# Attention of a graph network on one core: groups of four chunks in an order fixed by the source

## The chip, the core and the metric

The kernel runs on one core of a Trainium2 chip. A core has five engines, each with its own queue of instructions that it works off in order: TensorE (PE in the profile; PEld is its loading of weights), VectorE (DVE), ScalarE (ACT), GpSimd (POOL) and SyncE (SP). They wait for each other through semaphores. Data moves between the memory of the chip and the core's SBUF by DMA; transfers with an index per row (gathers) are issued by POOL, plain ones here by SP and ACT. The time is that of one execution on the device in microseconds, the median of several runs.

## The reference, cut to what matters

6250 nodes have 256 features each; 106,250 edges (50,000 drawn ones in both directions and a loop at each node) are sorted by destination. Two blocks follow each other, each with a layer norm and a relu ahead and a residual behind. The first is three layers of a relational network. The second, which the change touches, is graph attention:

```
h = x @ Wv + bv
q, k = h @ wq + bq, h @ wk + bk
e = q[src] + k[dst]
c = where(e > 0, e, 0.2 * e)
m = segment_max(c, dst);  ex = exp(c - m[dst])
attn = ex / segment_sum(ex, dst)[dst]
out = x + segment_sum(h[src] * attn[:, None], dst)
```

## The kernel before

The edges are cut into 831 chunks of 128. 56 windows of destination nodes take 15 chunks each (47 of them) or 14 (nine); a window holds at most 128 nodes, and the last chunk of the window in front is looked at again for the edges that spill over, so 15 or 16 chunks are used in a window (`refs`). If the input doesn't have the order that this needs, a general path runs instead; for this input `ordered_path` runs.

Three layers come first. In each, POOL gathers for every chunk the 128 source rows (`msg`, L719), DVE builds a 0/1 matrix of edge against node and type (`hot`), and TensorE sums with it (L852) and multiplies by the weights (L790). The last layer also leaves a table `hx` in memory: for each node its 256 values of `h` and its `q`.

Attention goes over the same chunks and windows with the line L719 gathering `head`, 128 rows of `hx`, 48 buffers deep. For a window:

- For each chunk DVE compares a row of numbers with the edges' local destinations (`other`, L911: 1 where the edge does not end at the node), ACT makes `qm` from it (L918: `other` times -1e30 plus `q` of the edge's source, so that edges of other nodes vanish in the exponent), and TensorE turns it (L920) so that nodes lie on partitions. Up to four chunks share a bank `pq` of PSUM, the accumulating memory; three such banks take turns.
- For each group of four: ACT writes 0.2 times the logits to `c` (L923), DVE takes the maximum into `tops` (L924) and puts the larger of the logit and its fifth into `c` (L925).
- Four small DVE steps make the guard of the exponent from `tops` (L928 to L931), then ACT takes the exponent of the whole window in one pass and sums it (L933).
- For each group: TensorE turns the weights back (`pe`, L938), DVE (even groups) or ACT (odd groups) copies them to SBUF (`ex`, L943 and L941), and TensorE multiplies them with the heads and sums over all chunks in `po` (L945; each of these matmuls is two passes in the profile).
- DVE divides by the sum and adds the window's rows of x (`y`, L951). SP loads those rows (`xt`, L916) and stores the result (L953), both at an address that it reads from `first`, a word which DVE writes after the first `other` of the window (`at_base`, L722 to L728).

The source says this window by window. The order of instructions on each engine isn't that of the source: a planner with assumed costs orders each stage by priority, and puts semaphores where data or buffers ask for them. In the order that it made for attention, the queues hold the `other` and `qm` of the next window between the parts of the present one, and on TensorE the turning back of three groups in a row, then their sums in one run of 24 passes, then the last group.

Of the kernel before, what the change touches and what calls it, by code (L numbers as in the profile page):

```python
# [19 lines left out]
P = 128  # L20
KS = 19
NO_NODE = 1 << 20
MASKED = -1.0e30
FLOOR = -1.0e29
EPS = 1e-5
SLOPE = 0.2
# [403 lines left out]
def kernel(  # L430
# [19 lines left out]
    nc = tc.nc  # L450
    N, D = x.shape
# [3 lines left out]
    HX = D + 1  # L455
# [3 lines left out]
    NW = -(-NC // CW)  # L459
# [3 lines left out]
    sizes = [CW] * NLONG + [CW - 1] * NS  # L463
    first_c = [sum(sizes[:t]) for t in range(NW)]
# [3 lines left out]
    groups = [list(range(g, min(g + 4, NT))) for g in range(0, NT, 4)]  # L468
# [33 lines left out]
    with tc.tile_pool(name="prep", bufs=1) as prep, \  # L502
# [49 lines left out]
        for at, view, k in by_window(dst_t):  # L552
# [36 lines left out]
        for to, of, b in ((loc_p, dst_t, base_b), (seg_p, seg_t, seg_b)):  # L589
# [15 lines left out]
                                op0=ALU.mult, op1=ALU.add)  # L605
        nc.vector.tensor_reduce(viol[:, 1:2], scr[:, :full], AX.X, ALU.max)
        if rest:
            nc.vector.tensor_copy(viol[:rest, 2:3], over[:rest, full:full + 1])
            nc.vector.tensor_scalar(viol[:rest, 3:4], seg[:rest, full:full + 1], -1.0, -0.5,
                                    op0=ALU.mult, op1=ALU.add)  # L610
# [17 lines left out]
                                op0=ALU.mult, op1=ALU.add)  # L628
# [39 lines left out]
    with tc.tile_pool(name="nw", bufs=3) as nw:  # L668
# [3 lines left out]
        for ts in groups:  # L672
            n = len(ts)
            xt = nw.tile([P, 4, D], F32, name="xt")
# [32 lines left out]
    def ordered_path():  # L707
# [5 lines left out]
        up = cps.tile([P, WMAX], F32)  # L713
        nc.vector.tensor_copy(up, up_s)
        k_n = cst.tile([P, NW], F32)
        bs = path.enter_context(tc.tile_pool(name="bs", bufs=3))

        def gather(to: bass.AP, table: bass.AP, index: bass.AP):
            nc.gpsimd.indirect_dma_start(  # L719
                out=to, out_offset=None, in_=table[:N, :],  # L720
                in_offset=bass.IndirectOffsetOnAxis(ap=index, axis=0))

        def at_base(t: int, after: bass.AP):

            first = bs.tile([1, 1], I32, name="first")
            nc.vector.scalar_tensor_tensor(first, after[0:1, 0:1], 0.0, base[:, t:t + 1],
                                           op0=ALU.mult, op1=ALU.add)
            return nc.sync.value_load(first[0:1, 0:1], min_val=0,  # L728
                                      max_val=N - P if t < NW - 1 else N - 1)

        with ExitStack() as s:
            wp = s.enter_context(tc.tile_pool(name="weights", bufs=2))
            mp = s.enter_context(tc.tile_pool(name="msgs", bufs=36))
# [99 lines left out]
            for l in range(L):  # L833
                nxt = load_weights(l + 1) if l + 1 < L else None
                ahead = None
                pending = None
                for t in range(NW):
                    n = sizes[t]
# [21 lines left out]
                    if ahead is not None:  # L860
                        hot = op.tile([P, R], BF16, name="hot_p", bufs=3)
                        nc.vector.tensor_scalar(hot, up[:, :R], seg_p[:, t:t + 1], None,
                                                op0=ALU.is_equal)
                        add(ahead, hot, 0, R)
                    for k in range(n):
                        c = first_c[t] + k
                        lo, hi = ranges[n][k]
                        msg = mp.tile([P, 3, D], BF16, name="msg")
# [5 lines left out]
                        ahead = msg  # L874
# [5 lines left out]
                weights = nxt  # L880

        with ExitStack() as s:
            mp = s.enter_context(tc.tile_pool(name="heads", bufs=48))
            ep = s.enter_context(tc.tile_pool(name="edges", bufs=6))
            cp = s.enter_context(tc.tile_pool(name="logits", bufs=2))
            rp = s.enter_context(tc.tile_pool(name="rows2", bufs=2))
            aps = s.enter_context(tc.tile_pool(name="aps", bufs=1, space=PSUM))
            NE = CW + 1
            ahead = None
            for t in range(NW):  # L890
                n = sizes[t]
                refs = [] if ahead is None else [(ahead, loc_p[:, t:t + 1])]
                for k in range(n):
                    c = first_c[t] + k
                    msg = mp.tile([P, HX], F32, name="head")
                    gather(msg, hx, src_t[:, c:c + 1])
                    refs.append((msg, loc[:, c:c + 1]))
                ahead = refs[-1][0]
                chunks = [list(range(g, min(g + 4, len(refs)))) for g in range(0, len(refs), 4)]
                sm = rp.tile([P, 8], F32, name="sm")  # L900
                k2 = sm[:, 0:1]
                k1 = k_n[:, t:t + 1]
                nc.vector.tensor_scalar_mul(k2, k1, SLOPE)

                c_t = cp.tile([P, NE * P], F32, name="c")
                tops = rp.tile([P, 4], F32, name="tops")
                for g, js in enumerate(chunks):
                    pq = aps.tile([P, 4, P], F32, name="pq", bufs=3)
                    for i, j in enumerate(js):
                        other = ep.tile([P, P], F32, name="other")  # L910
                        nc.vector.tensor_scalar(other, up[:, :P], refs[j][1], None,  # L911
                                                op0=ALU.not_equal)
                        if j == 0:
                            at = at_base(t, other)
                            xt = rp.tile([P, D], F32, name="xt")
                            nc.sync.dma_start(xt, xa[ds(at, P), :])  # L916
                        qm = ep.tile([P, P], F32, name="qm")
                        nc.scalar.activation(qm, other, AF.Identity, scale=MASKED,  # L918
                                             bias=refs[j][0][:, D:HX])
                        nc.tensor.transpose(pq[:, i, :], qm, ident)  # L920
                    flat = pq[:, :len(js), :].rearrange("p j e -> p (j e)")
                    to = c_t[:, js[0] * P:(js[-1] + 1) * P]
                    nc.scalar.activation(to, flat, AF.Identity, scale=SLOPE, bias=k2)  # L923
                    nc.vector.tensor_reduce(tops[:, g:g + 1], flat, AX.X, ALU.max)  # L924
                    nc.vector.scalar_tensor_tensor(to, flat, k1, to, op0=ALU.add, op1=ALU.max)  # L925
                ng = len(chunks)
                top, m2, neg, tot, inv = (sm[:, i:i + 1] for i in range(1, 6))
                nc.vector.tensor_reduce(top, tops[:, :ng], AX.X, ALU.max)  # L928
                nc.vector.tensor_scalar(m2, top, SLOPE, k2, op0=ALU.mult, op1=ALU.add)
                nc.vector.scalar_tensor_tensor(neg, top, k1, m2, op0=ALU.add, op1=ALU.max)  # L930
                nc.vector.tensor_scalar(neg, neg, FLOOR, -1.0, op0=ALU.max, op1=ALU.mult)  # L931
                w_ = len(refs) * P
                nc.scalar.activation(c_t[:, :w_], c_t[:, :w_], AF.Exp, bias=neg, accum_out=tot)  # L933
                po = aps.tile([P, D], F32, name="po")
                for g, js in enumerate(chunks):
                    pe = aps.tile([P, 4, P], F32, name="pe", bufs=3)
                    for i, j in enumerate(js):
                        nc.tensor.transpose(pe[:, i, :], c_t[:, j * P:(j + 1) * P], ident)  # L938
                    ex = ep.tile([P, 4, P], F32, name="ex", bufs=3)
                    if g % 2:  # L940
                        nc.scalar.copy(ex[:, :len(js), :], pe[:, :len(js), :])  # L941
                    else:
                        nc.vector.tensor_copy(ex[:, :len(js), :], pe[:, :len(js), :])  # L943
                    for i, j in enumerate(js):
                        nc.tensor.matmul(po, ex[:, i, :], refs[j][0][:, :D],  # L945
                                         start=(j == 0), stop=(j == len(refs) - 1))

                nc.vector.tensor_scalar_max(inv, tot, 1e-30)
                nc.vector.reciprocal(inv, inv)
                y = rp.tile([P, D], F32, name="y")  # L950
                nc.vector.scalar_tensor_tensor(y, po, inv, xt, op0=ALU.mult, op1=ALU.add)  # L951
                if t < NW - 1:
                    nc.sync.dma_start(out[ds(at, P), :], y)  # L953
                else:
                    nc.gpsimd.indirect_dma_start(  # L955
                        out=out, out_offset=bass.IndirectOffsetOnAxis(ap=last_i, axis=0),
                        in_=y, in_offset=None, bounds_check=N - 1, oob_is_err=False)

    unordered = nc.values_load(bad_i, min_val=0, max_val=1)
    with tc.If(unordered == 0) as cmp:  # L960
# [35 lines left out]
```

## Time and profile before

The median of three runs is 4491.3 us (4487.8 to 4492.2). The profile is of another, single execution under the profiler.

| what | value |
|---|---|
| median of the runs | 4491.3 us |
| the profiled execution's own time | 6330.7 us |
| its span, first to last instruction | 6328.4 us |
| mean granted clock of TensorE | 0.818 |
| TensorE busy | 4369.9 us, 69% of the span |
| VectorE busy | 2154.2 us, 34% |
| ScalarE busy | 1153.1 us, 18% |
| GpSimd busy | 3175.4 us, 50% |
| first gather of the layers, of attention | 146.9 us, 4628.9 us from the span's start |

The page lists groups of instructions by line: how many, their busy time and the mean duration of one, then how long the engine stood idle before them and what ended most of that. The timeline lists instructions in order of time; "x8" merges eight, and the bracket gives the idle time before and its releaser, where "remote" is one that no recorded event names. The table of stretches gives the busy time of each engine in a stretch of time, with the number of instructions, and the share of its clock that TensorE was granted. "L719" is a line of the kernel as it was before.

### The profile page before, as it was taken

What the parts mean: (1) busy time and instruction counts of PE and PEld (TensorE: products, weight loads), DVE (VectorE), ACT (ScalarE), POOL (GpSimd) and SP (SyncE); (2) the same over time, 40 slices, a digit from 0 to 9 for tenths busy, and PEclk for the clock granted to TensorE, in tenths of its full rate; (3) what the DMA queues carried; (4) which work ended last, traced back from release to release, by engine and by line L of the source; (5) the groups of instructions that cost most, each with busy time, mean ns of one, the idle gap of its engine ahead of it and who ended that gap; (6) DMA issues with size and microseconds to landing.
All of it is one profiled execution on the core that took longest, in us unless ns stands there. A gap on an engine that the chain in (4) does not pass through costs nothing. (4 is left out here: it accounts for less than half of the span.)

```text
span 6328.4 us, 79952 instructions
## 1 busy us (share of the span) xinstructions
PE 4369.9 (69%) x29260; PEld 3685.4 (58%) x29260; DVE 2154.2 (34%) x6241; ACT 1153.1 (18%) x2566; POOL 3175.4 (50%) x3411
## 2 busy tenths in 40 slices
PE   0687887888688788888868888888844454445545
PEld 0566666666566666666757777777733343334434
DVE  5222322223232222323223333333323433334434
ACT  2011111111011111111101111111123333333333
POOL 2555555555355555555355555555444444444443
PEclk5788988888788888888878888888966677667767
DMA  5544444444344444444344444444422222222221
GB/s 181 150 130 129 134 128 131 129 124 136 114 130 128 129 132 132 131 130 135 103 137 134 134 134 135 133 135 138 123 71 74 71 73 78 76 73 73 78 75 53
DMA packets 327774, 732.72 MB, mean 116 GB/s; under 512 B 65165, under 2 KB 181059, under 8 KB 327372
## 3 DMA queue, kind: packets, MB, share of 16 engines
q0 software_dynamic: 199536, 599.93, 34.4%
q1 hardware_dynamic: 117512, 118.48, 5.8%
q10 hardware_dynamic: 10324, 9.11, 0.5%
q8 instruction: 232, 3.80, 0.3%
q14 instruction: 170, 1.39, 0.1%
HBM read 652.42 MB, written 74.88 MB: 115 GB/s over the span
## 5 line engine op out<-in xcount | busy, mean ns | idle before, releaser
L719 POOL DMA_INDIRECT msg<-tab,src_t x2493 | 2355.8, 945 | 2062.7 <-PE bank L852 1060.1
L852 PE MATMUL bank<-hot,msg 128*128 128x104 bf16 (+16 forms) x17982 | 1725.4, 252 | 582.1 <-issue 416.9
L852 PEld LDWEIGHTS <-msg 128*128 128x128 bf16 x18972 | 1418.5, 102 | 896.7 <-issue 699.0
L790 PE MATMUL po<-wr,ag 128*128 128x256 f32 x5376 | 1533.4, 446 | 183.8 <-issue 165.4
L790 PEld LDWEIGHTS po<-wr,ag 128*128 128x128 f32 x5376 | 1381.2, 335 | 327.0 <-issue 226.5
L871 DVE TENSOR_SCALAR hot<-up,seg 128x104 bf16<-128x104 f32 (+10 forms) x2493 | 1017.0, 431 | 1398.9 <-PE bank L852 972.0
L719 POOL DMA_INDIRECT head<-hx,src_t x831 | 785.5, 945 | 895.6 <-PE po L945 452.8
L920 PE MATMUL pq<-ident,qm 128*128 128x128 f32 x886 | 221.9, 342 | 679.4 <-ACT qm L918 293.4
L784 ACT COPY ag<-bank 128x512 f32<-128x512 f32 x504 | 284.9, 587 | 1887.8 <-PE bank L852 1085.3
L920 PEld LDWEIGHTS pq<-ident,qm 128*128 128x128 f32 x886 | 130.6, 158 | 753.8 <-ACT qm L918 328.0
L795 DVE TENSOR_TENSOR po<-po,bb 128x256 f32<-128x256 f32 x168 | 72.7, 433 | 1270.7 <-PE po L793 1247.2
L945 PE MATMUL po<-head,ex 128*128 128x256 f32 x1772 | 457.3, 416 | 42.6 <-issue 30.6
L945 PEld LDWEIGHTS po<-head,ex 128*128 128x128 f32 x1772 | 368.3, 214 | 111.3 <-issue 41.3
L924 DVE TENSOR_REDUCE tops<-pq 128x1 f32<-128x512 f32 x224 | 153.0, 683 | 553.3 <-ACT c L923 340.2
L918 ACT ACTIVATE qm<-other,head 128x128 f32<-128x128 f32 x886 | 298.7, 394 | 119.5 <-issue 95.9
L938 PE MATMUL pe<-ident,c 128*128 128x128 f32 x886 | 190.6, 388 | 152.3 <-ACT c L933 142.7
L938 PEld LDWEIGHTS pe<-ident,c 128*128 128x128 f32 x886 | 162.5, 205 | 174.4 <-ACT c L933 158.5
L911 DVE TENSOR_SCALAR other<-up,loc 128x128 f32<-128x128 f32 x831 | 256.9, 340 | 11.1 <-ACT qm L918 10.8
L923 ACT ACTIVATE c<-pq,sm 128x512 f32<-128x512 f32 x224 | 150.1, 683 | 572.6 <-remote 472.2
L798 ACT ACTIVATE xs<-po 128x256 f32<-128x256 f32 x112 | 42.9, 383 | 988.8 <-DVE po L795 980.1
L818 PE MATMUL po<-wv_s,at 128*128 128x256 f32 x224 | 111.8, 652 | 159.6 <-ACT at L769 156.0
L782 DVE COPY ag<-bank 128x512 f32<-128x512 f32 x168 | 116.1, 691 | 273.6 <-remote 128.7
(135 smaller groups left out, 1844.2 us busy)
## 6 DMA issues: line engine op xcount, KB each, us to landing
msg<-tab,src_t POOLq DMA_INDIRECT x2493
xt<-xf SPq DMA_DIRECT2D x168, 128.0 KB
tab<-hml SPq DMA_DIRECT2D x112, 192.0 KB
xf<-xs SPq DMA_DIRECT2D x112, 128.0 KB
head<-hx,src_t POOLq DMA_INDIRECT x831
tab<-hml SPq DMA_DIRECT2D x12, 768.0 KB
hx<-row SPq DMA_DIRECT2D x56, 128.5 KB
xa<-x SPq DMA_DIRECT2D x56, 128.0 KB
```

Of the source, the lines that this page charges most:

```text
L719: nc.gpsimd.indirect_dma_start(out=to, out_offset=None, in_=table[:N, :], in_offset=bass.IndirectOffsetOnAxis(ap=index, axis=0))
L784: nc.scalar.copy(ag[:, h, half, :], banks[half][h])
L790: nc.tensor.matmul(po, by_r[:, r, :], wr[:, h, r, :], start=(r == 0 and h == 0), stop=False)
L852: nc.tensor.matmul(banks[b][h][:, a - b * SEG // 2:z - b * SEG // 2], w, hot[:, a - lo:z - lo], start=(not begun[b] and s_ == 0), stop=Fal ...
L871: nc.vector.tensor_scalar(hot[:, :R * (hi - lo)], up[:, :R * (hi - lo)], seg[:, c:c + 1], None, op0=ALU.is_equal)
L911: nc.vector.tensor_scalar(other, up[:, :P], refs[j][1], None, op0=ALU.not_equal)
L918: nc.scalar.activation(qm, other, AF.Identity, scale=MASKED, bias=refs[j][0][:, D:HX])
L920: nc.tensor.transpose(pq[:, i, :], qm, ident)
L923: nc.scalar.activation(to, flat, AF.Identity, scale=SLOPE, bias=k2)
L924: nc.vector.tensor_reduce(tops[:, g:g + 1], flat, AX.X, ALU.max)
L938: nc.tensor.transpose(pe[:, i, :], c_t[:, j * P:(j + 1) * P], ident)
L945: nc.tensor.matmul(po, ex[:, i, :], refs[j][0][:, :D], start=(j == 0), stop=(j == len(refs) - 1))
```

## The change

The attention stage is written anew. A switch turns the planner off for it (`manual_schedule`): each engine's instructions now stand in the order of the source. A window's chunks are in groups of four as before, and all groups of all windows make one list of 224 steps. A loop over this list does, in step i: the masking of group i (gathers, `qm`, transposes); at a window's beginning the exponent of the window that just ended; the sums of group i-6; the turning back of group i-5; the `other` of group i+1; the logits of group i, and after the last group of a window the guard. SP reads the address from `base_i`, a copy of all the windows' bases in whole numbers that is made once in the preparation, in place of `first`. Buffers: heads 56 for 48, edges 10 for 6, logits 3 for 2, rows 3 for 2. The arithmetic of a window is the same.

```diff
+    base_i = keep.tile([1, NW], I32)
...
+        nc.vector.tensor_copy(base_i, base)
...
-            mp = s.enter_context(tc.tile_pool(name="heads", bufs=48))
-            ep = s.enter_context(tc.tile_pool(name="edges", bufs=6))
-            cp = s.enter_context(tc.tile_pool(name="logits", bufs=2))
-            rp = s.enter_context(tc.tile_pool(name="rows2", bufs=2))
+            s.enter_context(tc.manual_schedule())
+            mp = s.enter_context(tc.tile_pool(name="heads", bufs=56))
+            ep = s.enter_context(tc.tile_pool(name="edges", bufs=10))
+            cp = s.enter_context(tc.tile_pool(name="logits", bufs=3))
+            rp = s.enter_context(tc.tile_pool(name="rows2", bufs=3))
...
+            GROUP = 4
...
+            def make_others(t: int, g: int):
+                w = wins[t]
+                others[t, g] = []
+                for j in w["groups"][g]:
+                    other = ep.tile([P, P], F32, name="other")
+                    nc.vector.tensor_scalar(other, up[:, :P], w["refs"][j][1], None,
+                                            op0=ALU.not_equal)
+                    others[t, g].append(other)
+
+            def begin_window(t: int):
+                w = wins[t]
+                at = nc.sync.value_load(base_i[0:1, t:t + 1], min_val=0,
+                                        max_val=N - P if t < NW - 1 else N - 1)
+                w["at"] = at
+                w["xt"] = rp.tile([P, D], F32, name="xt")
+                nc.sync.dma_start(w["xt"], xa[ds(at, P), :])
+                w["sm"] = rp.tile([P, 8], F32, name="sm")
+                nc.vector.tensor_scalar_mul(w["sm"][:, 0:1], k_n[:, t:t + 1], SLOPE)
...
+            def mask(t: int, g: int):
+                w = wins[t]
+                for j in w["groups"][g]:
+                    c = w["refs"][j][0]
+                    if c not in heads:
+                        heads[c] = mp.tile([P, HX], F32, name="head")
+                        gather(heads[c], hx, src_t[:, c:c + 1])
+                pq = aps.tile([P, GROUP, P], F32, name="pq", bufs=3)
+                for i, j in enumerate(w["groups"][g]):
+                    head = heads[w["refs"][j][0]]
+                    qm = ep.tile([P, P], F32, name="qm")
+                    nc.scalar.activation(qm, others[t, g][i], AF.Identity, scale=MASKED,
+                                         bias=head[:, D:HX])
+                    nc.tensor.transpose(pq[:, i, :], qm, ident)
+                w["pq"] = pq
...
+            def turn_back(t: int, g: int):
+                w = wins[t]
+                js = w["groups"][g]
+                pe = aps.tile([P, GROUP, P], F32, name="pe", bufs=3)
+                for i, j in enumerate(js):
+                    nc.tensor.transpose(pe[:, i, :], w["c"][:, j * P:(j + 1) * P], ident)
+                ex = ep.tile([P, GROUP, P], F32, name="ex", bufs=3)
+                if g % 2:
+                    nc.scalar.copy(ex[:, :len(js), :], pe[:, :len(js), :])
+                else:
+                    nc.vector.tensor_copy(ex[:, :len(js), :], pe[:, :len(js), :])
+                w["ex"] = ex
+
+            def weigh(t: int, g: int):
+                w = wins[t]
+                if g == 0:
+                    w["po"] = aps.tile([P, D], F32, name="po")
+                for i, j in enumerate(w["groups"][g]):
+                    nc.tensor.matmul(w["po"], w["ex"][:, i, :], heads[w["refs"][j][0]][:, :D],
+                                     start=(j == 0), stop=(j == len(w["refs"]) - 1),
+                                     skip_group_check=True)
...
+            LAG = 5
+            make_others(*steps[0])
+            for i in range(len(steps) + LAG + 1):
+                now = steps[i] if i < len(steps) else None
+                back = steps[i - LAG] if LAG <= i < len(steps) + LAG else None
+                sums = steps[i - LAG - 1] if i > LAG else None
+                if now and now[1] == 0:
+                    begin_window(now[0])
+                if now:
+                    mask(*now)
+                if 0 < i <= len(steps) and (i == len(steps) or now[1] == 0):
+                    exponents(steps[i - 1][0])
+                if sums:
+                    weigh(*sums)
+                if back:
+                    turn_back(*back)
+                if i + 1 < len(steps):
+                    make_others(*steps[i + 1])
+                if now:
+                    logits(*now)
+                    if i + 1 == len(steps) or steps[i + 1][1] == 0:
+                        guard(now[0])
```

`logits`, `guard` and `exponents` hold the lines of before for these parts, one group or one window at a time; the end of `weigh` holds `y` and its store.

More of the change, by code (lines that the diff above doesn't have):

```diff
@@ L887, in ordered_path @@
+            cp = s.enter_context(tc.tile_pool(name="logits", bufs=3))
+            rp = s.enter_context(tc.tile_pool(name="rows2", bufs=3))
             aps = s.enter_context(tc.tile_pool(name="aps", bufs=1, space=PSUM))
             NE = CW + 1
-            ahead = None
+            GROUP = 4
+            wins: list[dict] = []
+            steps = []
             for t in range(NW):
[L891 to L930, printed above, removed]
-                nc.vector.tensor_scalar(neg, neg, FLOOR, -1.0, op0=ALU.max, op1=ALU.mult)
[L932 to L946, printed above, removed]
@@ new lines, in ordered_path @@
+                cs = [first_c[t] + k for k in range(sizes[t])]
+                refs = ([] if t == 0 else [(cs[0] - 1, loc_p[:, t:t + 1])])
+                refs += [(c, loc[:, c:c + 1]) for c in cs]
+                groups_t = [list(range(g, min(g + GROUP, len(refs))))
+                            for g in range(0, len(refs), GROUP)]
+                wins.append({"refs": refs, "groups": groups_t})
+                steps += [(t, g) for g in range(len(groups_t))]
+            heads: dict[int, bass.AP] = {}
@@ new lines, in ordered_path @@
+            others: dict[tuple[int, int], list[bass.AP]] = {}
+            def make_others(t: int, g: int):
[15 more added lines that the diff above has]
+                nc.vector.tensor_scalar_mul(w["sm"][:, 0:1], k_n[:, t:t + 1], SLOPE)
+                w["c"] = cp.tile([P, NE * P], F32, name="c")
+                w["tops"] = rp.tile([P, 4], F32, name="tops")
@@ new lines, in logits @@
+            def logits(t: int, g: int):
+                w = wins[t]
+                js = w["groups"][g]
+                flat = w["pq"][:, :len(js), :].rearrange("p j e -> p (j e)")
+                to = w["c"][:, js[0] * P:(js[-1] + 1) * P]
+                nc.scalar.activation(to, flat, AF.Identity, scale=SLOPE, bias=w["sm"][:, 0:1])
+                nc.vector.tensor_reduce(w["tops"][:, g:g + 1], flat, AX.X, ALU.max)
+                nc.vector.scalar_tensor_tensor(to, flat, k_n[:, t:t + 1], to, op0=ALU.add,
+                                               op1=ALU.max)
@@ new lines, in guard @@
+            def guard(t: int):
+                w = wins[t]
+                top, m2, neg = (w["sm"][:, i:i + 1] for i in range(1, 4))
+                nc.vector.tensor_reduce(top, w["tops"][:, :len(w["groups"])], AX.X, ALU.max)
+                nc.vector.tensor_scalar(m2, top, SLOPE, w["sm"][:, 0:1], op0=ALU.mult, op1=ALU.add)
+                nc.vector.scalar_tensor_tensor(neg, top, k_n[:, t:t + 1], m2, op0=ALU.add,
+                                               op1=ALU.max)
+                nc.vector.tensor_scalar(neg, neg, FLOOR, -1.0, op0=ALU.max, op1=ALU.mult)
@@ L948, in ordered_path, with exponents @@
+            def exponents(t: int):
+                w = wins[t]
+                n = len(w["refs"]) * P
+                neg, tot, inv = (w["sm"][:, i:i + 1] for i in range(3, 6))
+                nc.scalar.activation(w["c"][:, :n], w["c"][:, :n], AF.Exp, bias=neg,
+                                     accum_out=tot)
                 nc.vector.tensor_scalar_max(inv, tot, 1e-30)
                 nc.vector.reciprocal(inv, inv)
+            def turn_back(t: int, g: int):
+                w = wins[t]
+                js = w["groups"][g]
+                pe = aps.tile([P, GROUP, P], F32, name="pe", bufs=3)
[7 more added lines that the diff above has]
+                w["ex"] = ex
@@ new lines, in weigh @@
+            def weigh(t: int, g: int):
+                w = wins[t]
+                if g == 0:
[4 more added lines that the diff above has]
+                                     skip_group_check=True)
+                if g < len(w["groups"]) - 1:
+                    return
@@ L950, in ordered_path @@
                 y = rp.tile([P, D], F32, name="y")
-                nc.vector.scalar_tensor_tensor(y, po, inv, xt, op0=ALU.mult, op1=ALU.add)
+                nc.vector.scalar_tensor_tensor(y, w["po"], w["sm"][:, 5:6], w["xt"],
+                                               op0=ALU.mult, op1=ALU.add)
                 if t < NW - 1:
-                    nc.sync.dma_start(out[ds(at, P), :], y)
+                    nc.sync.dma_start(out[ds(w["at"], P), :], y)
                 else:
```

## The prediction

> **What bounds the kernel now.** I read the page first: its span, and the gathers, which are the only work that has the same count in all four stages (three layers, then attention).
>
> ```profile
> span 6328.4 us, 79952 instructions
> ...
> L719 POOL DMA_INDIRECT msg<-tab,src_t x2493 | 2355.8, 945 | 2062.7 <-PE bank L852 1060.1
> ...
> L719 POOL DMA_INDIRECT head<-hx,src_t x831 | 785.5, 945 | 895.6 <-PE po L945 452.8
> ```
>
> The span, and the profiled execution's own 6330.7, lie 1,840 us over the 4491.3 of the runs. So something in this page is not in the runs, and it must be found before anything is summed. The timeline of one attention window (times from the span's start) shows it:
>
> ```profile
> 5339.59 1.99 PE L945 MATMUL po<-head,ex 128*128 128x256 f32 x8
> ...
> 5341.42 1.16 PE L920 MATMUL pq<-ident,qm 128*128 128x128 f32 x5
> ...
> 5343.05 0.95 POOL L719 DMA_INDIRECT head<-hx,src_t  x1 [0.30 <-issue]
> 5344.30 0.95 POOL L719 DMA_INDIRECT head<-hx,src_t  x1 [0.30 <-issue]
> ...
> 5349.98 0.49 DVE L951 SCALAR_TENSOR_TENSOR y<-po,sm,xt 128x256 f32<-128x256 f32 x1 [8.47 <-remote]
> ...
> 5354.23 0.69 ACT L923 ACTIVATE c<-pq,sm 128x512 f32<-128x512 f32 x1 [12.04 <-remote]
> ```
>
> The last matmul into `po` is over at 5341.6, the load of `xt` was issued at 5319.3, yet `y`, which needs only these two and a scalar, starts at 5349.98; `c` needs transposes over at 5342.6 and starts at 5354.2. Nothing recorded ends either wait, and it recurs in nearly every window (330 us over 48 waits for `y`). I take it for TensorE's completions reaching the others late under the profiler. Without it a window of 31 us is some 18.5 us of chain. What isn't stretched is the gathers: whenever POOL is free to run, one starts each 1.25 us, in the layers and here (5343.05, 5344.30). Test that against the runs with the waits of the gathers' line and the list of waits:
>
> ```profile
>   DMA tab<-hml: 107.0, 2
>   DMA hx<-row: 46.1, 1
> ...
> POOL out_dram L955 <- POOLq L960: 57.0, 1, 57.0
> ```
>
> First gather at 146.9; 4 x 830 x 1.25 = 4150; three stage borders 57.1 + 51.8 + 64.9 (from one stage's last gather to the next one's first: the two waits for `tab`, the one for `hx`, and the stray gather of `x`) = 173.8; tail 58. Sum 4529, the median's 4491 plus 0.9%, with the borders and the tail still holding some of the lateness. So in the runs all four stages go at POOL's pace of 1.25 us a gather: attention's 831 take 1038 us, 18.55 us a window, and its chain hides behind them. Every number below is therefore a difference to 4491.3; 6330.7 can't carry a sum. About 0.2% is what this kernel's runs can tell from no change.
>
> **The change, part by part.**
>
> *What it removes.* Per window one 1x1 write of `first` (L726, 0.14 us of DVE) and its wait; `base_i` costs one tiny copy in the preparation. DVE's 14 us of work a window lie under 18.55 of gathers: nothing. SP's value load, load of `xt` and store of `y` stay one each; now the loads for the next window stand ahead of this window's store. `xt` has some nine steps until `y` needs it (30 us before), and three buffers; nothing either way, and if that cover went, a few us a window at most.
>
> *What it moves.* The gathers are recorded in mask(), in the old order, and POOL's queue held nothing else, so nothing moves on POOL. 56 head buffers for 48 let it run 10 us further ahead: worthless if the end is set elsewhere. Counts of matmuls, activations and DVE passes stay the same. What changes is who stands behind whom. Each step of four chunks now has on TensorE: four transposes of step i, the eight passes of weigh (step i-6), four transposes back (i-5). On DVE: copy of `ex` (even groups), the four `other` of step i+1, `tops`, `c`. On ACT: four `qm`, at a window's start the exponent, copy of `ex` (odd groups), `c`.[...]
>
> *The new wait.* The copy of `ex` waits for transposes that stand behind weigh, which stands behind transposes that wait for `qm`; behind the copy on DVE stand the four `other`, for which the next `qm` wait (and on ACT, behind its copy, `c` and the next `qm`). So within a step everything is one ring, and nothing of the next step's masking starts before this step's sums are through. Length of the ring at full clock, from rows of the timeline: four `qm`, three at 0.29 apart and one of 0.39, 1.27; hop to TensorE 0.05 (5326.14 to 5326.20); the last transpose 0.11 (four took 0.60, i.e. 0.11 apart and 0.27 the last); weigh 8 x 0.216 = 1.73 (eight took 1.99 with a slow first); transposes back 0.60; hop 0.05; copy of `ex` on DVE 0.61 (0.69 less what the next overlaps); first `other` 0.34; hop 0.05. Sum 4.81 us. With the copy on ACT, 0.48 + 0.58 for `c` in place of 0.61 + 0.34 + 0.05: 4.87. `y` fits between weigh and the copy. At a window's start the exponent waits for the guard: `c` of the last group 0.69, hop, `tops` 0.61, `c` on DVE 0.74, four scalar steps 0.9, less the 0.58 that ACT has used: 2.41 after the first `qm`; then hop 0.05, exponent 1.98, copy 0.48, `c` 0.58: 5.50. A window has four steps in either size: 5.50 + 4.81 + 4.87 + 4.81 = 20.0 us, against 18.55 of gathers. The gathers no longer set the pace.
>
> *The clock.* In the ring the matmuls are 2.6 us of about 5, so what TensorE is granted counts in full, which it didn't while it was hidden. At half clock the pitches are 0.213 for a transpose (twelve in 2.82) and 0.43 for a pass: +0.10, +1.71 and +0.51, so 7.1 a step, 28.6 a window. Which clock? Consecutive stretches of 3.41 us in the first layer (columns: length; busy us of TensorE, its weight loads, DVE, ACT, POOL; granted clock; DMA):
>
> ```profile
> 2289.10:2292.51 3.41, 1.94 (x19) 1.43 (x16) 0.48 (x1) 0.00 (x0) 2.51 (x3) 1.00 0.86 237
> 2292.51:2295.93 3.42, 2.79 (x31) 2.05 (x30) 1.71 (x6) 1.07 (x2) 1.88 (x2) 1.00 0.42 118
> 2295.93:2299.34 3.41, 1.04 (x9) 0.64 (x9) 0.39 (x1) 0.00 (x0) 2.50 (x4) 1.00 0.66 198
> 2299.34:2302.75 3.41, 2.00 (x6) 1.01 (x5) 0.75 (x2) 0.58 (x1) 1.34 (x3) 0.50 0.55 163
> 2302.75:2306.17 3.42, 3.14 (x8) 2.52 (x8) 1.69 (x5) 0.38 (x1) 2.79 (x3) 0.50 0.35 88
> 2306.17:2309.58 3.41, 3.41 (x16) 3.39 (x16) 0.00 (x0) 0.00 (x0) 0.95 (x1) 1.00 0.49 143
> ...
> 2394.91:2398.33 3.42, 1.92 (x14) 0.98 (x12) 0.48 (x1) 0.00 (x0) 2.22 (x3) 1.00 0.76 250
> 2398.33:2401.74 3.41, 2.78 (x13) 1.90 (x14) 1.71 (x6) 1.07 (x2) 1.89 (x2) 0.50 0.42 115
> ```
>
> A stretch with 1.04 busy is followed by half clock, one with 1.94 isn't, one with 1.92 is; at half clock 2.00 doesn't bring the full one back, 3.14 does. [...]from the last transpose back (3.76 after the first `qm`) to the next step's first transpose the gap is 1.5 us in most steps and 2.2 at a window's start, which leaves 1.9 and 1.2 us busy in the emptiest stretch, on the edge and beyond it. At half clock weigh and the transposes back alone fill 4.5 us on end, so a stretch or two later the clock is back. I take the rows, since they are this chip at this kind of load: one drop a window, back after one to two steps, 45% of the steps at half clock: 20.0 + 0.45 x 8.6 = 23.9 us a window. The ends are 20.0 and 28.6.
>
> *Sum.* Before: 1038 + a tail of 58 with two late completions of some 12 each taken off: 1070 from the first head gather. After: 2.9 for the first gather to reach ACT (4628.9 to 4631.8) and three more gathers 3.7, 56 windows, and six steps of emptying without masking at some 2.8: 23 + 56 x 23.9 = 1361. Difference +291: 4491 + 291 = 4782, said as 4780.
>
> **The rivals.**
> *Full clock throughout*[...]: 23 + 1120 = 1143, +73, 4565. [...]Against it: the rows above.
> *Mostly half clock*: 23 + 56 x 28.6 = 1625, 5045. For it: attention in the page's strip shows a PEclk of 6 to 7 tenths. Against: a slow step fills a stretch, and 3.14 busy brought full clock back.
> *Hidden anyway*: the ring takes under 4.6 us a step, and the gathers go on setting the pace: 4491, or 4480 with a shorter tail. It would need the hops and the four `other` to cost nothing (0.2 + 0.34 off 4.87 still isn't enough), so it is unlikely.
> *Faster*: part of POOL's waits for `po` (452.8) and `qm` is real in the runs, that is, the planner's attention goes at its chain and not at the gathers, with `y` at the head of DVE's queue holding up `tops` and `c`. The total then asks for a shorter gather pace in the layers: at 1.20, three layers take 2988, with 147 + 174 before and between them, which leaves 1182 for attention, 21 a window. The ring at full clock would take 1143: 4452. It decides where the window of before is over 20 us in the runs; the fit of 1.25 to the total speaks against it.
>
> **How the numbers follow.** Ring with a changing clock 0.60 (own range 4680 to 4870), full clock 0.20, half clock 0.08, hidden 0.06, faster 0.06. The range reaches down to the full clock's 4565 and up over the likeliest's end: 4560 to 4880. Slower by over 0.2% takes the first three and nothing else: 0.88; same 0.06; faster 0.06.
>
> **What would show it.** In the changed kernel's profile: on TensorE 4, 8, 4 matmuls a step from `mask`, `weigh`, `turn_back`; its first transpose of a step ended by `qm`, `qm` by `other` in every second step; gathers waiting on `weigh`'s matmuls for the whole stage, not its first part; stretches of attention changing between 1.00 and 0.50 about once a window. Its span isn't forecast, since late completions will stretch it too. The forecast is wrong if gathers run at 1.25 without waits, if the clock stays full, or if steps are nearer 4.5 us than 5 to 7.

## The result, and the profile after

The changed kernel takes 4752.5 us (median of four runs, 4748.7 to 4760.2), the kernel before 4489.6 beside it (4486.6 to 4492.2): a ratio of 1.0588, with an interval of 1.0570 to 1.0606. It is slower by 263 us; 4780 had been forecast, 291 above the runs before, with a range of 4560 to 4880.

On one chip used here the kernel before takes 6330 us in plain runs too, as in its first profile, with waits that no recorded event ends (the prediction takes them for late completions of TensorE, which no run shows); the first four experiments fell on that chip, and all others, like the profile of the changed kernel, did not.

The page of the changed kernel, cut to its span, the clock granted to TensorE (tenths, 40 slices), and the groups of the attention stage:

```profile
span 4747.4 us, 79970 instructions
...
PEclk9999999999899999999999999999777788877878
...
L721 POOL DMA_INDIRECT msg<-tab,src_t x2493 | 2357.6, 946 | 812.4 <-issue 409.4
...
L721 POOL DMA_INDIRECT head<-hx,src_t x831 | 785.3, 945 | 552.5 <-PE po L994 293.8
...
L994 PE MATMUL po<-head,ex 128*128 128x256 f32 x1772 | 619.0, 513 | 5.5 <-ACT ex L984 3.1
L943 PE MATMUL pq<-ident,qm 128*128 128x128 f32 x886 | 275.4, 346 | 374.9 <-ACT qm L941 374.9
...
L941 ACT ACTIVATE qm<-other,head 128x128 f32<-128x128 f32 x886 | 284.3, 393 | 400.1 <-DVE other L912 369.0
```

This execution took 4749.6 us itself, so it stands for the runs as it is, which the first profile of before did not. Attention begins where the strip of the clock falls from 9 to 7 and 8. The gathers of the layers hardly change (812 us idle beside 2358 busy; 816 and 2364 in e9, the kernel before without such waits), but those of `head` wait for `po`, that is for weigh, for 294 us (65 in e9). And `qm` waits for `other` for 369 us: the next step's masks come too late, as the ring of the prediction has them.

The rows of one line or tile give shortest, median and longest duration in ns, and then the first and the last start:

```profile
L721 POOL DMA_INDIRECT head<-hx,src_t x831: 940/946/958, 3377.6 to 4669.8; - x167
```

```profile
L1000 DVE SCALAR_TENSOR_TENSOR y<-po,sm,xt x56: 482/484/485, 3433.5 to 4739.9; 128x256 f32<-128x256 f32 x56
```

`y` comes once a window. From the first to the last there are 55 windows in 1306.4 us, 23.75 us each, and from the first head gather to the end of the last store's issue, the last work in the chain (4741.6), 1364 us pass. The prediction had 23.9 and 1361.

For the other side of the comparison the kernel before had to be profiled where it takes 4490 us (experiment e9 below); its own time was 4498.9 us:

```profile
L719 POOL DMA_INDIRECT head<-hx,src_t x831: 943/949/963, 3390.6 to 4437.7; - x167
```

```profile
L951 DVE SCALAR_TENSOR_TENSOR y<-po,sm,xt x56: 474/484/488, 3430.4 to 4488.8; 128x256 f32<-128x256 f32 x56
```

Here the gathers take 1047.1 us, 18.7 a window, and `y` 19.2 a window; attention ends in the same way at 4490.6, 1100 us after its first gather. So the difference lies in attention: 1364 - 1100 = 264, for 263 in the runs. That it agrees to 1 us is partly chance. In the layers this execution of before was 13 us slower than the changed kernel's (first head gather at 3391 and 3378), though their source is the same, and it was itself 7 us above the median of the runs beside it.

### The profile page after: what moved, and what is told of

The parts are those of the page before. It is cut to its first block, busy times and chain, and to the rows that moved or that the text cites. A ratio compares the mean times of both kernels' runs of the same rounds, so it can differ in the third digit from the quotient of the medians.

```text
span 4747.4 us, 79970 instructions
## 1 busy us (share of the span) xinstructions
PE 4025.7 (85%) x29260; PEld 3548.3 (75%) x29260; DVE 2149.8 (45%) x6186; ACT 1155.8 (24%) x2566; POOL 3176.9 (67%) x3411
## 5 line engine op out<-in xcount | busy, mean ns | idle before, releaser
L854 PE MATMUL bank<-hot,msg 128*128 128x104 bf16 (+16 forms) x17982 | 1485.1, 240 | 273.6 <-DMA msg<-tab,src_t 141.4
L854 PEld LDWEIGHTS <-msg 128*128 128x128 bf16 x18972 | 1348.9, 98 | 414.4 <-DMA msg<-tab,src_t 189.1
L792 PE MATMUL po<-wr,ag 128*128 128x256 f32 x5376 | 1344.4, 409 | 0.1
L792 PEld LDWEIGHTS po<-wr,ag 128*128 128x128 f32 x5376 | 1307.8, 337 | 5.6 <-ACT ag L786 0.8
L994 PE MATMUL po<-head,ex 128*128 128x256 f32 x1772 | 619.0, 513 | 5.5 <-ACT ex L984 3.1
L943 PE MATMUL pq<-ident,qm 128*128 128x128 f32 x886 | 275.4, 346 | 374.9 <-ACT qm L941 374.9
L994 PEld LDWEIGHTS po<-head,ex 128*128 128x128 f32 x1772 | 446.6, 263 | 84.8 <-ACT ex L984 3.8
L912 DVE TENSOR_SCALAR other<-up,loc 128x128 f32<-128x128 f32 x831 | 232.6, 340 | 0.0
L771 ACT ACTIVATE at<-pt 128x256 f32<-128x256 f32 x224 | 85.9, 383 | 408.0 <-PE pt L769 398.7
L795 PE MATMUL po<-wo,at 128*128 128x256 f32 x672 | 172.4, 379 | 0.0
```

The lines of the kernel that those rows point to most:

```text
L792: nc.tensor.matmul(po, by_r[:, r, :], wr[:, h, r, :], start=(r == 0 and h == 0), stop=False)
L795: nc.tensor.matmul(po, x_t[:, h, :], wo[:, h, :], start=False, stop=(h == KH - 1))
L854: nc.tensor.matmul(banks[b][h][:, a - b * SEG // 2:z - b * SEG // 2], w, hot[:, a - lo:z - lo], start=(not begun[b] and s_ == 0), stop=Fal ...
L912: nc.vector.tensor_scalar(other, up[:, :P], w["refs"][j][1], None, op0=ALU.not_equal)
L994: nc.tensor.matmul(w["po"], w["ex"][:, i, :], heads[w["refs"][j][0]][:, :D], start=(j == 0), stop=(j == len(w["refs"]) - 1), skip_group_ch ...
```

## The experiments

Three questions were put. Is the loss the ring? How much of it is the ring's own length, and how much the clock? And is anything in the change worth having once the ring is gone? Twelve kernels were run; e0 to e3 on the chip where the kernel before takes 6330 us, and therefore three of them again.

| kernel | edit | before beside it | us | ratio (95%) |
|---|---|---|---|---|
| e1 | planner's order | 6330.4 | 5920.9 | 0.9348 (0.9319 to 0.9378) |
| e2 | filler matmuls | 6330.4 | 5985.2 | 0.9452 (0.9423 to 0.9482) |
| e3 | `other` first | 6330.4 | 6012.6 | 0.9495 (0.9465 to 0.9524) |
| e5 | the changed kernel itself | 4490.1 | 4756.6 | 1.0596 (1.0578 to 1.0613) |
| e6 | as e2 | 4490.1 | 4547.6 | 1.0135 (1.0118 to 1.0151) |
| e7 | as e3 | 4490.1 | 4548.0 | 1.0136 (1.0119 to 1.0153) |
| e8 | copies one step later | 4490.1 | 4448.8 | 0.9912 (0.9895 to 0.9928) |
| e10 | as e1 | 4491.8 | 4450.5 | 0.9910 (0.9894 to 0.9927) |
| e11 | before, with the buffers of after | 4493.2 | 4460.6 | 0.9925 (0.9908 to 0.9941) |
| e12 | e8 with 48 head buffers | 4493.2 | 4453.0 | 0.9908 (0.9892 to 0.9925) |

**e0, the kernel before once more.** No edit.

> The kernel before, unchanged, profiled once more. The late completions of its first profile were taken as something that the runs don't have. If so, and if they don't come back here, the span is about 4490 us, the gathers of attention stand 1.25 us apart throughout, 830 of them in 1038 us, and the layers' likewise. If the waits for y and c belong to the kernel, the span is again far above the runs' median and attention's gathers take some 1630 us.

It took 6347.8 us, and plain runs without a profile beside it 6330.4 (seven, 6313.9 to 6352.6). The page's span, and two of the waits with their sum, count and longest:

```profile
span 6345.5 us, 79952 instructions
```

```profile
ACT c L923 <- remote: 518.7, 56, 13.5
...
DVE y L951 <- remote: 333.5, 45, 11.3
```

These are the waits that nothing recorded ends, the same that the first profile showed. As plain runs take the same time, they are not the profiler's doing. Nearly all waits of this kind in e0 are for something that TensorE writes or reads, in the layers too; late completions of TensorE fit that, but no run shows the completions themselves.

**e1, the planner's order for the changed source.** The fixed order is taken off; a value load of `base_i` needs that order, so the window's base comes as it did before.

```
-            s.enter_context(tc.manual_schedule())
-                at = nc.sync.value_load(base_i[0:1, t:t + 1], ...)
+                at = at_base(t, others[t, 0][0])
```

> The changed source, but ordered by the planner: the switch manual_schedule is taken out (and the address comes by the old at_base again, since the planner would load all addresses at once). Buffers, groups and arithmetic stay those of the change. Theory of the ring (the fixed order makes the 263 us): the planner puts other and qm into the gaps again, the gathers set the pace, 4470 to 4500 us. Rival (the new grouping, its buffers or where the gathers are recorded cost the time): it stays near 4750.

6.5% faster than before on that chip: attention, from the first head gather to the end of the span, takes 1310 us for 1714 in e0.

**e2, matmuls that keep TensorE busy.** Work is added, the output is the same: eight transposes of the identity in each step, into the bank that the step's own transposes overwrite, put where TensorE would wait for `qm`.

```
+            FILL = 8
...
+                for i in range(FILL):
+                    nc.tensor.transpose(pq[:, i % GROUP, :], ident, ident)
                 for i, j in enumerate(w["groups"][g]):
...
                     nc.tensor.transpose(pq[:, i, :], qm, ident)
```

> The changed kernel with eight more transposes in every step, of the identity into the bank that the step's real transposes then overwrite, placed on TensorE ahead of them, that is in the gap in which it waits for qm (0.9 us at full clock, gap 1.5 to 2.2). Work is added, the ring is not shortened. Theory (ring of 20.0 us a window at full clock, the rest is the clock that falls to half in the gaps): the clock stays full, the emptiest stretch has 2 us and more busy, 4550 to 4590 us. Rival (the clock is incidental, the ring itself is 23 us): no gain, 4750 or more; eight transposes at half clock take 1.7 us and would then lengthen steps, to 4800 and over.

**e3, the next step's `other` ahead of the copy of `ex`.**

```
-                if back:
-                    turn_back(*back)
                 if i + 1 < len(steps):
                     make_others(*steps[i + 1])
+                if back:
+                    turn_back(*back)
```

> The changed kernel with one pair of calls exchanged: make_others of the next step stands ahead of turn_back, so on DVE the four other are no longer behind the copy of ex. The ring is cut in the steps whose copy is on DVE (two of four), not in those whose copy is on ACT. Theory: the next qm are ready when TensorE gets there, 3.6 us in the cut steps and the ones after them shorter by the 1.2 of their qm, some 16 to 17 us a window at full clock, below the 18.55 of the gathers: 4490 us if the clock stays full, up to 4600 with drops to half clock. Rival (the ring is long through weigh and the clock, not through other behind the copy): a few us a step less at most in two of four steps, 4700 and over.

Both are faster than before there, by 5.5% and 5.1% (attention 1365 and 1396 us for 1714). On that chip before loses more than these variants do, which says nothing about the question asked, so they were run again.

**e5, the changed kernel beside its variants.** No edit.

> The changed kernel itself, beside the kernel before on one chip. The first four experiments ran where TensorE's completions reach the other engines late in plain runs too (before: 6330 us); its own result was taken where they don't (4490 and 4753). If before takes 4490 here: 4753 again. If before takes 6330 here: its attention is then set by a chain with late completions and not by the gathers (1699 us from the first gather of heads to the end), and the change's shorter runs of matmuls between hand-overs make up for its ring: 1400 to 1500 us for attention, 6030 to 6130, so faster than before there. If lateness only adds the same to both, it stays slower than before by some 260 us.

4756.6, 266.5 us above before; a window takes 23.85 us. The variants below are held against this.

**e6, the filler again.**

> The changed kernel with eight more transposes a step (work added in the gap on TensorE), now on the same chip as the changed kernel itself. Where completions are in time: 4550 to 4590 us if the clock is what lengthens the ring from 20.0 us a window, 4750 or more if it isn't. Where they are late: under the changed kernel by some 50 to 150 us for the same reason, since the granted clock in attention was then 0.9 and more.

4547.6, at the edge of what was expected: the filler takes 209 us off. Attention in stretches of 500 us, first the changed kernel, then this one (length; busy us of TensorE, its weight loads, DVE, ACT, POOL, with counts; granted clock; DMA share, GB/s):

```profile
3900.00:4400.00 500.00, 368.35 (x1317) 260.88 (x1317) 249.94 (x697) 217.95 (x493) 290.43 (x308) 0.80 0.33 92
```

```profile
3900.00:4400.00 500.00, 415.16 (x2350) 322.22 (x2349) 294.61 (x827) 257.35 (x585) 345.86 (x367) 1.00 0.40 110
```

TensorE does more instructions (2350 for 1317), the clock is 1.00 for 0.80, and POOL issues 367 gathers in the time of 308. A window takes 20.1 us (the line of `y` below), the 20.0 that the prediction gave the ring at full clock. Of the loss 57.5 us stay. They are what the ring's own length costs, less what the change gains elsewhere: above e8, the same source without the ring, e6 lies by 98.8 us.

```profile
L1003 DVE SCALAR_TENSOR_TENSOR y<-po,sm,xt x56: 482/484/485, 3430.2 to 4535.8; 128x256 f32<-128x256 f32 x56
```

**e7, `other` first, again.**

> The changed kernel with make_others ahead of turn_back, on the same chip as the changed kernel itself. Where completions are in time: 4490 to 4600 us if the other behind the copy of ex are a link of the ring, 4700 and over if the ring hangs on something else. Where they are late: under the changed kernel by 50 us and more.

4548.0, 20.07 us a window, with the clock at 0.90 in attention. An estimate from that is 0.2 x 20.07 = 4.0 us a window at half clock, about one drop of 3.41 us, where the changed kernel has some 2.6 drops. The window is not as short as was expected of it (16 to 17 us). Three things in the trace stand against it: in a window's second step `y`, which waits for weigh, stands ahead of `other` on DVE; ACT's copy of `ex` is in two of four steps still; and the exponent waits for the guard:

```profile
ACT c L970 <- DVE sm L964: 172.1, 55, 5.7
```

How the 209 us divide between a shorter ring and a steadier clock isn't settled by this run.

**e8, the ring cut.** turn_back is split: it transposes only, and the copy of its result to `ex` comes one step later, behind that step's masks, the sums another step later. The matmuls that the copy waits for are then a whole step old. The loop runs one step longer; nothing else is changed.

```
                 back = steps[i - LAG] ...
-                sums = steps[i - LAG - 1] if i > LAG else None
+                copy = steps[i - LAG - 1] if LAG < i <= len(steps) + LAG else None
+                sums = steps[i - LAG - 2] if i > LAG + 1 else None
...
+                if copy:
+                    copy_back(*copy)
                 if sums:
                     weigh(*sums)
```

> The changed kernel with the copy of ex taken out of turn_back and placed one step later, behind that step's mask (the sums go one step later with it). Neither other on DVE nor c and qm on ACT stand behind a copy that waits for this step's TensorE: the ring is cut in all four steps. Where completions are in time: TensorE's 2.6 us a step at full clock or 5.2 at half and ACT's 3.1 lie beside each other, the gathers set the pace again, 4470 to 4500 us, not slower than before; with one copy more in flight the drain is one step longer. Rival (the clock alone makes the change slow): it falls to half all the more with larger gaps, 4600 and over. Where completions are late: under the others, 5900 or less.

4448.8: 308 us less than the changed kernel, and 41 less than before, which is also some 20 less than was expected; e9 to e12 ask where these come from. Its gathers on the page, by first and last start, and the last wait of its end:

```profile
L721 POOL DMA_INDIRECT head<-hx,src_t x831 | 785.7, 945 | 298.2 <-PE pq L943 63.4
```

```profile
L721 POOL DMA_INDIRECT head<-hx,src_t x831: 942/946/962, 3378.5 to 4416.1; - x167
```

```profile
POOL out_dram L1011 <- POOLq L1044: 21.7, 1, 21.7
```

1037.6 us for 830 gaps is 1.250 each: POOL never waits for a buffer (45.4 of the 298 us idle are the wait for `hx` at the start, the other 253 are 0.30 between two gathers). The clock still falls at times (it is 0.88 over 3900 to 4400), and the gathers don't notice, because TensorE is off the path again.

**e9, the kernel before where it takes 4490 us.** No edit; its rows stand in the section above.

> The kernel before, unchanged, profiled where the runs take 4490 us, if this chip is such a one. Forecast from the prediction: attention's gathers 1.25 us apart, 1038 us in all, and no wait for y or c that nothing recorded ends. Since the kernel with late copies takes 41 us less than before with gathers at exactly that pace, the 41 us must be somewhere: either before's gathers wait after all (about 1075 us for them) or they don't and its tail after the last gather is some 65 us against 24. If this chip has late completions (6330), the profile is as the first one.

```profile
POOL out_dram L955 <- POOLq L960: 50.9, 1, 50.9
```

No wait of the kind without a recorded end is in its list. POOL is at its pace almost to the end (1047.1 us, less 1037.5, leaves 10), but the chain of a window takes 19.2 us and falls behind the gathers by half a microsecond a window; the head buffers hold the arrears, and they come out as a tail of 51 us. In e8 that tail is 22. The stretch of 500 us that stands above for the changed kernel shows one thing more:

```profile
3900.00:4400.00 500.00, 366.74 (x1647) 300.23 (x1647) 308.41 (x910) 271.19 (x619) 374.90 (x396) 0.80 0.44 119
```

The granted clock is 0.80 here too, as in the changed kernel. So the change did not lower the clock; it put TensorE on the path, where the same clock costs time. (e11 below has 0.81 there and runs at the gathers' pace.)

**e10, the planner again.**

> The changed source ordered by the planner (the switch for the fixed order taken out, the address by the old at_base), again, now beside a before that takes 4490 us, if this chip is such a one. Theory of the ring: 4450 to 4500 us, as before or with the late copies, since the groups, buffers and arithmetic of the change cost nothing. Rival (they do, and the order isn't all): over 4550. Where completions are late: 5920 again, against 6330.

4450.5, 41 us less than before: the changed source in the planner's order does what the ring-free fixed order does.

```profile
L721 POOL DMA_INDIRECT head<-hx,src_t x831: 942/946/965, 3382.1 to 4419.6; - x167
```

**e11, the buffers alone.** The kernel before with the buffer numbers of the changed one (the edit in short).

```
-  heads 48, edges 6, logits 2, rows2 2
+  heads 56, edges 10, logits 3, rows2 3
```

> The kernel before, its order left to the planner, with the four buffer numbers of the changed kernel (56 heads, 10 edges, 3 logits, 3 rows). It asks which part of the changed source is worth the 41 us that the changed kernel gains once its ring is cut. If it is the buffers (before's chain of 19.2 us a window shortens to the gathers' pace of 18.6 when the planner may run further ahead): some 4450, head gathers over 1038 us, tail 21 to 25 us. If it is the recorded order and the grouping: within 10 us of before, gathers 1047, tail 50.

4460.6, 32.5 less than before. Its head gathers, and its tail:

```profile
L719 POOL DMA_INDIRECT head<-hx,src_t x831: 941/947/960, 3389.1 to 4427.2; - x167
```

```profile
POOL out_dram L955 <- POOLq L960: 27.1, 1, 27.1
```

1038.1 us and 27: both nearly those of e8. So some four fifths of the 41 us are the buffers.

**e12, e8 with 48 heads** (in short).

```
-  heads 56
+  heads 48
```

> The changed kernel with its copies of ex one step later (4449 us in the earlier run), and with 48 head buffers in place of 56; nothing else differs. The prediction called the 56 worthless where the end is set elsewhere. If so, 4449 within 5 us, gathers at 1.25 us with hardly a wait for a buffer. If the eight buffers carry it: this order holds a head for one step longer (four to five heads more), gathers wait on weigh's matmuls, and it takes 4460 to 4500.

4453.0, 40 us less than before, as e8 is 41. The eight head buffers are worth nothing that can be measured in this order. If that holds in the planner's order too, which was not tried, the gain of e11 is in the others (masks, logits, rows); which of them was not tried either.

## Why the prediction was right, and where it was not

**The first profile of before does not stand for the runs: right; its reason: wrong.** The lateness was put down to the profiler. e0 has it in plain runs, and e9 is a profile without it. What these waits come from stays open. The forecast of the changed kernel that its own span would be stretched did not come true either: 4749.6 for 4752.5.

**The pace of the gathers: right.** 1.25 us a gather held wherever nothing kept POOL waiting: e8 and e10 ran 831 of them in 1037.6 and 1037.5 us, where the prediction had 1038. (Its sum of 4529 lies 0.8% above the median, not 0.9.)

**Before's chain at 18.5 us, hidden: mis-sized.** It is 19.2, just over the gathers' 18.55. Buffers hid the difference until the end, so the term "1070 from the first head gather" is 1100. That is a small piece of the rival "faster", whose mechanism (before goes at its chain) was real and worth most of the 41 us of e8 (32.5 of them in e11). But it needed the ring to be gone; its price was worked out with the ring at full clock and a gather pace of 1.20, and neither was so.

**The ring: right, link by link.** The timeline of the changed kernel around a window's start:

```profile
4001.31 1.27 ACT L941 ACTIVATE qm<-other,head 128x128 f32<-128x128 f32 x4
...
4001.77 1.20 PE L943 MATMUL pq<-ident,qm 128*128 128x128 f32 x4 [1.55 <-ACT qm L941]
...
4002.80 2.98 PE L994 MATMUL po<-head,ex 128*128 128x256 f32 x8
...
4005.58 1.06 PE L981 MATMUL pe<-ident,c 128*128 128x128 f32 x4
...
4006.68 0.69 DVE L986 COPY ex<-pe 128x512 f32<-128x512 f32 x1 [3.87 <-PE pe L981]
4007.28 0.34 DVE L912 TENSOR_SCALAR other<-up,loc_p 128x128 f32<-128x128 f32 x1
...
4007.72 1.28 ACT L941 ACTIVATE qm<-other,head 128x128 f32<-128x128 f32 x4 [4.03 <-DVE other L912]
...
4009.21 1.90 PE L994 MATMUL po<-head,ex 128*128 128x256 f32 x8
...
4013.49 1.27 ACT L941 ACTIVATE qm<-other,head 128x128 f32<-128x128 f32 x4
...
4019.48 1.28 ACT L941 ACTIVATE qm<-other,head 128x128 f32<-128x128 f32 x4 [3.47 <-DVE other L912]
```

Read down: masks, transposes, weigh, transposes back, copy of `ex`, `other`, next masks, each at once behind the one above it; DVE stands still for 3.87 us in front of the copy, and ACT for 4.03 in front of the masks. From `qm` to `qm` the steps take 6.41, 5.77 and 5.99 us, where a step at full clock had been put at 4.81 to 5.50 and one at half clock at 7.1. The first has weigh partly at half clock (2.98 us for 1.90 in the second). That this ring, and not the grouping, is the loss is shown by e8: with the one hand-over moved by a step, all of it is gone.

The rival "hidden anyway" was put aside by a sum that doesn't hold: 0.2 + 0.34 off 4.87 leaves 4.33, which is under the 4.6 asked for, and the 0.34 of `other` isn't part of the 4.87 at all. What rules it out is e6: at full clock a window still takes 20.1 us, above the 18.55 of the gathers.

**The clock: the rows were read right; the form of the drop was mis-sized.** Consecutive stretches of 3.41 us of the changed kernel (columns as in the prediction):

```profile
3996.59:4000.00 3.41, 3.41 (x11) 2.60 (x10) 1.10 (x5) 0.00 (x0) 1.89 (x2) 0.50 0.16 43
4000.00:4003.42 3.42, 1.87 (x9) 1.15 (x8) 1.35 (x2) 2.75 (x7) 1.90 (x2) 1.00 0.38 100
4003.42:4006.83 3.41, 3.22 (x10) 2.24 (x9) 0.15 (x1) 0.27 (x1) 2.05 (x3) 0.50 0.18 54
4006.83:4010.24 3.41, 2.07 (x9) 1.51 (x10) 3.32 (x10) 1.28 (x4) 1.73 (x2) 1.00 0.41 116
4010.24:4013.66 3.42, 1.31 (x9) 0.92 (x7) 1.27 (x8) 3.22 (x5) 2.46 (x3) 1.00 0.20 51
4013.66:4017.07 3.41, 3.13 (x9) 2.45 (x10) 1.54 (x4) 1.78 (x5) 1.48 (x3) 0.50 0.36 106
4017.07:4020.48 3.41, 1.88 (x10) 1.21 (x9) 2.47 (x7) 1.00 (x4) 2.67 (x3) 1.00 0.40 105
4020.48:4023.89 3.41, 2.83 (x15) 2.14 (x14) 1.98 (x6) 0.83 (x3) 1.24 (x2) 1.00 0.30 88
```

1.87 and 1.31 busy are followed by half clock, 2.07 is not; 3.41, 3.22 and 3.13 busy at half clock are followed by full clock. The longest gap between two TensorE instructions from 3440 to 4730 is 2.39 us, so the clock fell here without a longer one. The edge isn't sharp. The 1.88 near the end is followed by full clock; from 3440 to 4730, 121 of the 139 stretches with 1.85 to 1.90 busy at full clock were followed by half clock, and none of the 65 with 2.00 or more. With the filler (e6), whose clock is 1.00 over 3900 to 4400, a stretch with 1.91 is followed by full clock:

```profile
3997.64:4001.06 3.42, 1.91 (x16) 1.57 (x14) 1.47 (x7) 3.42 (x7) 2.81 (x3) 1.00 0.39 112
4001.06:4004.47 3.41, 3.41 (x20) 2.70 (x20) 1.70 (x4) 1.37 (x4) 2.50 (x4) 1.00 0.38 99
```

Recorded busy time alone doesn't settle it, and what else counts stays open. That the clock would stay full throughout, at 0.20 in the forecast, was the author's estimate.

"One drop a window, back after one to two steps" became 147 drops in 56 windows (3378 to 4747), mostly of a single stretch each. That the window came out at 23.75 us for 23.9 is partly luck. The forecast's 45% counts steps; as steps at half clock are longer, it means 0.45 x 28.6 of 23.9 us, 54% of the time. Measured was 39% of the time (147 of the 377 stretches from 3440 to 4730). But each us at half clock cost more: (23.75 - 20.1) / (0.39 x 23.75) = 0.39 us, where the forecast has 8.6 / 28.6 = 0.30. Less half clock at a higher price gave nearly the same.

**The sum: 291 for 263, from errors that are named.** Attention after: 1361 forecast, 1364 measured; 55 windows took 1306 for 1315, and filling and emptying with the other window 58 for 47, which cancel. Attention before: 1070 forecast, 1100 measured. This error of 30 makes the excess of 28 us. The ends were right as well: the 20.0 us a window forecast for full clock stand beside e6's 20.1, and its 4547.6 stands near the 4565 of the rival "full clock". On one chip, then, the 266.5 us are 209 that go with the drops of the clock and 98.8 that the ring costs at full clock, less the 41.3 that e8 gains over before.

**Costed at nothing.** Gathers and SP's queue: right. The 56 heads: right in the ring-free order (e12). The buffers as a whole: wrong. The prediction looked at the other ones for `xt` alone, and found no wait; e11 shows that all four numbers together are worth 32.5 us in the planner's order, which the ring swallowed. The remaining 8 us to e10 (grouping, or what the planner makes of it) were not taken apart.

**Signs.** The counts of 4, 8, 4 matmuls a step, `qm` behind `other`, gathers behind weigh, and the clock changing between 0.50 and 1.00 all came; only "about once a window" did not.

Not tried: the changed kernel itself where the kernel before takes 6330 us. Its three variants beat before there by 5 to 6.5%, so it may well do so too, but no run shows it.

## What to carry to other kernels

In an order fixed by hand, look for the instruction that waits for this step's work and stands ahead of the next step's producers on the same engine: such a copy made one ring of all engines here, and moving it by a step was worth 308 us, more than the whole loss. With TensorE on the ring, a half clock that was hidden before (0.80 granted in both kernels) cost time, and its price (209 us) was twice that of the ring's own length (99); filler matmuls told the two apart. Before a trace is summed, hold its own time against the timed runs, and where they differ, profile again before taking a chain for hidden.

## What the hardware showed that had not been expected

In the changed kernel's attention the clock fell to half 144 times from 3440 to 4730, though no gap between TensorE instructions there was longer than 2.39 us. None of the 65 stretches of 3.41 us with 2.00 or more of recorded TensorE work at full clock was followed by half clock, and 121 of the 139 with 1.85 to 1.90 were; with the filler one with 1.91 was followed by full clock. Work that computes nothing, 8 transposes in each step, made the kernel 209 us faster.

The same kernel takes 4490 us on three chips and 6330 on a fourth, in runs that agree among themselves to within 0.4% of their median; on the fourth it has waits that no recorded event ends, for `c` alone 519 us in 56 waits of up to 13.5. Their cause was not found.
